# Selective scan with feed-forward: rows of B through HBM, rows of C by row quarters, a projection in column tiles, an interleaved input

## The chip, the cores and the metric

The kernel runs on one NeuronCore of a Trainium2 chip. The metric is device time in microseconds of one execution. A profile is one execution recorded instruction by instruction. TensorE (PE) does matrix products, VectorE (DVE), ScalarE (ACT) and GpSimd (POOL) work element by element, SyncE (SP) issues DMAs. SBUF is the on-chip memory of 128 partitions, PSUM the accumulator memory [...].

## What is computed

A block over x of shape (2, 1024, 512): RMS norm, a selective mask, low-rank projections, a state-space recurrence with N = 128 states for each of D = 512 features, an output projection, a layer norm, then a gated feed-forward of width 2048 and a second layer norm. All is fp32. The reference, cut:

```python
xn = x * rsqrt(mean(x * x) + 1e-06) * norm_w
xn = xn * sigmoid((xn @ select_proj_w.T + select_proj_b) * select_gate)
xp = xn @ x_proj_w.T                      # delta, B_ssm, C_ssm: 128 each
delta = softplus(xp[..., :R] @ dt_proj_w.T + dt_proj_b)
A = -exp(A_log)
h = exp(dt[:, :, None] * A) * h + (dt * xt)[:, :, None] * bt[:, None, :]   # for each token
y = einsum('bdn,bn->bd', h, ct)
x = layernorm(x + (y + x * D_param) @ out_proj_w.T)
x = layernorm(x + (silu(x @ w_gate.T) * (x @ w_up.T)) @ w_down.T)
```

## The kernel before

The 2048 tokens are cut into four chunks of T = 512 tokens, two for each sequence. For a chunk, `pre` (L114) makes the operands of the scan with features on the partitions: `xT`, `dt`, `u` = dt times the normed input, each [128, 4, 512] (the 512 features are NM = 4 groups of 128), and `b_sb`, `c_sb`, [128, 512], whose partitions are the state indices. `scan` (L212) goes through the 128 state indices n one at a time. For each n:

- `feed` (L228) is called one index ahead. `spread` (L220) puts row n of `b_sb` on all 128 partitions by a matmul with column n of the identity, broadcast, as stationary operand (L223), into the only bank of `ps_b`; ScalarE copies it to `bs` (L231); GpSimd multiplies `u` by it to make `bu` (L233), which has three buffers.
- `step` (L235) spreads row n of `c_sb` the same way into the only bank of `ps_c`. For each of the four feature groups ScalarE makes a = exp(dt times A) into PSUM (L240, two banks) and VectorE runs the recurrence along the 512 tokens with a scan instruction, in place in `bu` (L241). If another chunk of the sequence follows, GpSimd keeps the last column as state (L247). VectorE multiplies all four groups by the row of C to make `hc` (L249, two buffers).
- `reduce` (L251) is called one index late: four matmuls with the identity add `hc` to `y` (L254) in four PSUM banks.

An fp32 product appears in the profile as two MATMUL instructions and two weight loads.

After every second index one step of the neighbouring chunks' work is taken: `post` of the chunk before (L193: output projection L200, residual L203, statistics L204, layer norm L182-L191), then `pre` of the chunk after. Their PSUM tiles come from `ps_b` as well, under the same tag `b`. The calls state dependences; the framework orders the instructions of each engine from them, and every engine works its own queue in order, so that a waiting instruction holds those queued behind it. The last chunk's `post` runs alone after the scan (L305).

The feed-forward then takes the chunks in turn: `ffn_in` (L311) transposes the tokens of a chunk into `x1T` on TensorE (L110) with a copy by ScalarE (L111); for each of the 16 groups of hidden features 4 + 4 products make `pg` and `pu` (L325), whose moving operand is a row of 512 elements of `x1T`; SiLU (L329) and a product (L330) make `h`; then the down projection (L337), residual, layer norm and store. The weights `wg`, `wu`, `wd` arrive by DMA from L288, L299 and L300.

Of the kernel before, what the change touches and what calls it, by code (L numbers as in the profile page):

```python
# [9 lines left out]
FP = mybir.dt.float32  # L10
# [2 lines left out]
PSUM = bass.MemoryType.PSUM  # L13

P = 128
T = 512  # tokens of a chunk
RMS_EPS = 1e-6
LN_EPS = 1e-5
# columns of `vecs`, in groups of one column per 128 features
V_NORM, V_SELB, V_GATE, V_DTB, V_D = range(5)  # L20


# [1 line left out]
def kernel(  # L24
# [62 lines left out]
    def col(group, m):  # L87
        return vec[:, group, m : m + 1]

    # A = -exp(A_log)  # L90
    nc.scalar.activation(neg_a, neg_a, AF.Exp)
    nc.vector.tensor_scalar_mul(neg_a, neg_a, -1.0)
    nc.vector.tensor_tensor(gate_b, vec[:, V_SELB, :], vec[:, V_GATE, :], ALU.mult)
# [2 lines left out]
    state = chunk.tile([P, NM, N], FP, name="state", bufs=1)  # L96
    scan_pool = tc.alloc_tile_pool(name="scan", bufs=2)
    ps_y = tc.alloc_tile_pool(name="ps_y", bufs=1, space=PSUM)
    ps_b = tc.alloc_tile_pool(name="ps_b", bufs=1, space=PSUM)
    ps_c = tc.alloc_tile_pool(name="ps_c", bufs=1, space=PSUM)  # L100
    ps_a = tc.alloc_tile_pool(name="ps_a", bufs=2, space=PSUM)

    made = {}

    def transposed(dst, src, pool, tag, name):
        """dst[:, m, j*P:] = transposes of the blocks of src [P, NT, D]; one step for each m."""
        for m in range(NM):
            ps = pool.tile([P, T], FP, tag=tag, name=f"{name}_{m}")
            for j in range(NT):
                nc.tensor.transpose(ps[:, ts(j, P)], src[:, j, ts(m, P)], ident)  # L110
            nc.scalar.copy(dst[:, m, :], ps)  # L111
            yield

    def pre(c):  # L114
        """From the tokens of a chunk to the scan's operands, features on the partitions."""
        xT = chunk.tile([P, NM, T], FP, tag="xT", name=f"xT_{c}")
        dt = chunk.tile([P, NM, T], FP, tag="dt", name=f"dt_{c}")
        u = chunk.tile([P, NM, T], FP, tag="u", name=f"u_{c}")
        b_sb = chunk.tile([P, T], FP, tag="b_sb", name=f"b_sb_{c}")
        c_sb = chunk.tile([P, T], FP, tag="c_sb", name=f"c_sb_{c}")  # L120
        xn = pre_pool.tile([P, NM, T], FP, tag="xn", name=f"xn_{c}")
        rms = pre_pool.tile([P, T], FP, tag="rms", name=f"rms_{c}")
        low = pre_pool.tile([P, T], FP, tag="low", name=f"low_{c}")
        made[c] = xT, dt, u, b_sb, c_sb

        yield from transposed(xT, xc[c], ps_b, "b", f"tr_{c}")

        # RMS norm: a product with ones sums the squares and spreads the sum over the partitions
        nc.gpsimd.tensor_tensor(xn, xT, xT, ALU.mult)
        ps = ps_b.tile([P, T], FP, tag="b", name=f"ss_{c}")  # L130
        for k in range(NM):
            nc.tensor.matmul(ps, ones, xn[:, k, :], start=(k == 0), stop=(k == NM - 1))
        nc.scalar.activation(rms, ps, AF.Sqrt, bias=eps_r, scale=1.0 / D)
        yield
        nc.vector.reciprocal(rms, rms)
        for m in range(NM):
            nc.vector.scalar_tensor_tensor(  # L137
                xn[:, m, :], xT[:, m, :], col(V_NORM, m), rms, ALU.mult, ALU.mult
            )
        yield  # L140

        # selective mask
        for m in range(NM):
            ps = ps_b.tile([P, T], FP, tag="b", name=f"sel_{c}_{m}")
            for k in range(NM):
                nc.tensor.matmul(  # L146
                    ps, sel_w[:, k, ts(m, P)], xn[:, k, :], start=(k == 0), stop=(k == NM - 1)
                )
            nc.scalar.activation(
                dt[:, m, :], ps, AF.Identity, bias=gate_b[:, m : m + 1], scale=col(V_GATE, m)  # L150
            )
            yield
        nc.scalar.activation(dt, dt, AF.Sigmoid)
        nc.gpsimd.tensor_tensor(xn, xn, dt, ALU.mult)
        yield

        # low-rank delta, B and C
        for g, dst in enumerate((low, b_sb, c_sb)):
            ps = ps_b.tile([P, T], FP, tag="b", name=f"xp_{c}_{g}")
            for k in range(NM):  # L160
                nc.tensor.matmul(
                    ps, xp_w[:, k, ts(g, P)], xn[:, k, :], start=(k == 0), stop=(k == NM - 1)
                )
            nc.scalar.copy(dst, ps)
            yield

        # softplus(z) = max(z, 0) + ln(1 + exp(-|z|))
        for m in range(NM):
            ps = ps_b.tile([P, T], FP, tag="b", name=f"z_{c}_{m}")
            nc.tensor.matmul(ps, dt_w[:, ts(m, P)], low, start=True, stop=True)  # L170
            nc.scalar.activation(u[:, m, :], ps, AF.Relu, bias=col(V_DTB, m))
            nc.scalar.activation(dt[:, m, :], ps, AF.Abs, bias=col(V_DTB, m))
            yield
        nc.scalar.activation(dt, dt, AF.Exp, scale=-1.0)
        nc.scalar.activation(dt, dt, AF.Ln, bias=ones[:, 0:1])
        nc.gpsimd.tensor_tensor(dt, dt, u, ALU.add)
        nc.gpsimd.tensor_tensor(u, dt, xn, ALU.mult)  # L177
        yield

    def layernorm(t, stats, name):  # L180
        """Over the free dim of each of the NT rows of t, in place, from their bn_stats."""
        mv = small.tile([P, NT, 2], FP, tag="mv", name=f"mv_{name}")  # L182
        for j in range(NT):
            nc.vector.bn_aggr(mv[:, j, :], stats[:, j, :])
# [6 lines left out]
            )  # L191

    def post(c, pool, tag):  # L193
        """Output projection, residual and layer norm; the chunk's tile of x takes the result."""
        z = made[c][0]
        stats = small.tile([P, NT, 6], FP, tag="stats", name=f"stats_a{c}")
        for j in range(NT):
            ps = pool.tile([P, T], FP, tag=tag, name=f"op_{c}_{j}")
            for k in range(NM):
                nc.tensor.matmul(  # L200
                    ps, z[:, k, ts(j, P)], out_w[:, k, :], start=(k == 0), stop=(k == NM - 1)
                )
            nc.vector.tensor_tensor(xc[c][:, j, :], xc[c][:, j, :], ps, ALU.add)  # L203
            nc.vector.bn_stats(stats[:, j, :], xc[c][:, j, :])  # L204
            yield
        layernorm(xc[c], stats, f"a{c}")
        yield
# [2 lines left out]
        return t.unsqueeze(1).to_broadcast([P, NM, T])  # L210

    def scan(c, others):  # L212
        """The recurrence over a chunk, one state index at a time; `others` are steps of the
        neighbouring chunks' work, taken along the way."""
        xT, dt, u, b_sb, c_sb = made[c]
        first, last = c % CPB == 0, c % CPB == CPB - 1
        y = [ps_y.tile([P, T], FP, tag=f"y{m}", name=f"y_{c}_{m}") for m in range(NM)]
        bus, hcs = {}, {}

        def spread(pool, tag, src, n):  # L220
            """Row n of src on all partitions."""
            ps = pool.tile([P, T], FP, tag=tag, name=f"{tag}_{c}_{n}")
            nc.tensor.matmul(  # L223
                ps, ident[:, n : n + 1].to_broadcast([P, P]), src, start=True, stop=True
            )
            return ps

        def feed(n):  # L228
            ps = spread(ps_b, "b", b_sb, n)
            bs = scan_pool.tile([P, T], FP, tag="bs", name=f"bs_{c}_{n}")  # L230
            nc.scalar.copy(bs, ps)  # L231
            bus[n] = scan_pool.tile([P, NM, T], FP, tag="bu", name=f"bu_{c}_{n}", bufs=3)
            nc.gpsimd.tensor_tensor(bus[n], u, wide(bs), ALU.mult)  # L233

        def step(n):  # L235
            bu = bus.pop(n)
            cp = spread(ps_c, "c", c_sb, n)
            for m in range(NM):
                a = ps_a.tile([P, T], FP, tag="a", name=f"a_{c}_{n}_{m}")
                nc.scalar.activation(a, dt[:, m, :], AF.Exp, scale=neg_a[:, m, n : n + 1])  # L240
# [4 lines left out]
                )  # L245
            if not last:
                nc.gpsimd.tensor_copy(state[:, :, n], bu[:, :, T - 1])  # L247
            hcs[n] = scan_pool.tile([P, NM, T], FP, tag="hc", name=f"hc_{c}_{n}")
            nc.vector.tensor_tensor(hcs[n], bu, wide(cp), ALU.mult)  # L249

        def reduce(n):  # L251
            hc = hcs.pop(n)
            for m in range(NM):
                nc.tensor.matmul(y[m], ident, hc[:, m, :], start=(n == 0), stop=(n == N - 1))  # L254

        feed(0)
        for n in range(N):
            if n + 1 < N:
                feed(n + 1)
            step(n)  # L260
            if n:
                reduce(n - 1)
            if n % 2 and others:
                if next(others[0], "end") == "end":
                    others.pop(0)
        reduce(N - 1)
        for g in others:
            for _ in g:
                pass
        # z = y + x * D, in the place of x  # L270
        for m in range(NM):
            nc.vector.scalar_tensor_tensor(
                xT[:, m, :], xT[:, m, :], col(V_D, m), y[m], ALU.mult, ALU.add
# [15 lines left out]
        scan(c, others)  # L289

    ps_a.release()
    ps_c.release()
    ps_b.release()
    ps_y.release()
    scan_pool.release()
# [13 lines left out]
    ffn = ctx.enter_context(tc.tile_pool(name="ffn", bufs=2))  # L309

    def ffn_in(c):  # L311
        xT = ffn.tile([P, NM, T], FP, tag="x1T", name=f"x1T_{c}")
        for _ in transposed(xT, xc[c], ps_t, "t", f"tr1_{c}"):
            pass
        return xT
# [85 lines left out]
```

## Times and profile before

| what | value |
|---|---|
| runs without profile | 4687.51 and 4688.35 us, median 4687.93 |
| profiled execution: span, first to last instruction | 4687.7 us (no other time of that execution is recorded) |
| granted TensorE clock, mean | 0.952 |
| busy: PE, DVE, ACT, POOL | 3802.7, 3688.7, 1867.9, 2418.8 us |
| scan instructions on VectorE, L241 | 2048, 1168.3 + 1236.0 us (without and with a carried state) |
| `hc`, L249 | 512, 1166.4 us, 2278 ns each |
| `bu`, L233, on GpSimd | 512, 2312.9 us, 4521 ns each |
| `bs`, L231, on ScalarE | 512, 298.6 us, 583 ns each |
| spread of B and of C, L223 | 1024 instructions each, 573.8 and 603.0 us |
| HBM traffic | read 20.20 MB, written 4.19 MB |

How to read it: a line of a group gives line, engine, operation, names, count, busy time, mean of one in ns, and the idle time before these instructions with what ended it. A line of the timeline gives start and length in us, engine, line, operation and count, and in brackets the idle time before and its cause. A line of waits gives who waited for whom: sum in us, times, longest. The two rows of slices cut the span into 40 equal parts of 117 us; a digit is the busy share in tenths. The busy time of TensorE is modelled and overlaps; rates are better read from the starts.

### The profile page before, as it was taken

How to read it: one execution, taken by the hardware profiler on the slowest of the kernel's cores; microseconds unless marked ns; L12 is line 12 of the kernel's file. 1: busy time of each engine (PE TensorE's matmuls, PEld its weight loads, DVE VectorE, ACT ScalarE, POOL GpSimd, SP SyncE). 2: the span in 40 equal slices, each digit the busy share in tenths (PEclk: the TensorE clock that was granted, in tenths of full speed). 3: DMA queues.
4: the chain of work that ended last, by engine and by line, in shares of the span. 5: the costliest groups of instructions: out<-in, count | busy, mean ns of one | idle time of the engine just before them, and what ended most of it. 6: DMA issues, size and time to landing. Idle time of an engine off the chain costs nothing.

```text
span 4687.7 us, 25093 instructions
## 1 busy us (share of the span) xinstructions
PE 3802.7 (81%) x8224; PEld 1573.4 (34%) x8224; DVE 3688.7 (79%) x2798; ACT 1867.9 (40%) x2780; POOL 2418.8 (52%) x793
## 2 busy tenths in 40 slices
PE   5787777777787777787777777778788888999999
PEld 2333333333333333333333333333333333444444
DVE  1967999998877999998778999989999999211111
ACT  3434444443344444444345444434444444100000
POOL 3556666664545766655557666646666666000000
PEclk7988999998888999998899999989999999999999
DMA  1000000000000000000000000000000000100000
GB/s 65 0 0 0 0 0 0 0 0 0 0 0 0 0 0 0 0 0 0 0 0 36 0 0 0 0 0 0 0 0 0 0 0 0 72 9 0 9 9 9
DMA packets 9491, 25.99 MB, mean 6 GB/s; under 512 B 400, under 2 KB 912, under 8 KB 8336
## 3 DMA queue, kind: packets, MB, share of 16 engines
q1 hardware_dynamic: 9360, 24.39, 1.4%
q8 instruction: 64, 1.05, 0.1%
q14 instruction: 67, 0.55, 0.0%
HBM read 20.20 MB, written 4.19 MB: 5 GB/s over the span
## 4 chain that ended last, share of the span: by engine, by line
DVE 36%; PE 25%; issue 21%; POOL 15%; ACT 3%; DMA 0%; POOLq 0%; DVEq 0%; SPq 0%; ACTq 0%
DVE bu L241 28%; POOL bu L233 14%; DVE hc L249 6%; PE y L254 6%; PE po L337 5%; PE pg L325 5%; PE pu L325 5%; PE c L223 2%; ACT bs L231 1%; PE b L223 1%; ACT a L240 0%; PE sel L146 0%; DVE xc L189 0%; DVE xn L137 0%; POOL u L177 0%
## 5 line engine op out<-in xcount | busy, mean ns | idle before, releaser
L233 POOL TENSOR_TENSOR bu<-u,bs 128x2048 f32<-128x2048 f32 x512 | 2312.9, 4521 | 1307.8 <-ACT bs L231 735.2
L240 ACT ACTIVATE a<-dt,neg_a 128x512 f32<-128x512 f32 x2048 | 1415.6, 692 | 1854.1 <-DVE bu L241 1851.2
L254 PE MATMUL y<-hc,ident 128*128 128x512 f32 x4096 | 1931.7, 615 | 5.7 <-DVE hc L249 5.7
L241 DVE TENSOR_TENSOR_SCAN bu<-a,bu 128x512 f32<-128x512 f32 x1024 | 1168.3, 1202 | 225.0 <-POOL bu L233 224.6
L241 DVE TENSOR_TENSOR_SCAN bu<-a,state,bu 128x512 f32<-128x512 f32 x1024 | 1236.0, 1263 | 106.0 <-POOL bu L233 99.1
L249 DVE TENSOR_TENSOR hc<-bu,c 128x2048 f32<-128x2048 f32 x512 | 1166.4, 2278 | 36.1 <-PE c L223 1.2
L254 PEld LDWEIGHTS y<-hc,ident 128*128 128x128 f32 x4096 | 819.1, 200 | 1072.3 <-issue 1063.3
L223 PE MATMUL c<-c_sb,ident 128*128 128x512 f32 x1024 | 603.0, 672 | 586.5 <-DVE hc L249 586.0
L223 PE MATMUL b<-b_sb,ident 128*128 128x512 f32 x1024 | 573.8, 644 | 219.1 <-ACT bs L231 93.2
L223 PEld LDWEIGHTS c<-c_sb,ident 128*128 128x128 f32 x1024 | 167.3, 196 | 973.4 <-DVE hc L249 933.5
L231 ACT COPY bs<-b 128x512 f32<-128x512 f32 x512 | 298.6, 583 | 260.2 <-PE b L223 224.7
L223 PEld LDWEIGHTS b<-b_sb,ident 128*128 128x128 f32 x1024 | 198.3, 201 | 498.0 <-issue 206.1
L330 DVE TENSOR_TENSOR h<-sg,pu 128x512 f32<-128x512 f32 x64 | 44.0, 687 | 383.0 <-PE pu L325 383.0
L325 PE MATMUL pg<-x1T,wg 128*128 128x512 f32 x512 | 230.5, 592 | 0.0
L325 PE MATMUL pu<-x1T,wu 128*128 128x512 f32 x512 | 230.3, 592 | 0.0
L337 PE MATMUL po<-wd,h 128*128 128x512 f32 x512 | 220.9, 592 | 0.0
L329 ACT ACTIVATE sg<-pg 128x512 f32<-128x512 f32 x64 | 38.2, 597 | 376.9 <-PE pg L325 376.9
L340 DVE TENSOR_TENSOR xc<-xc,po 128x512 f32<-128x512 f32 x16 | 11.0, 688 | 202.4 <-PE po L337 202.4
L325 PEld LDWEIGHTS pu<-x1T,wu 128*128 128x128 f32 x512 | 97.3, 190 | 122.5 <-issue 122.5
L325 PEld LDWEIGHTS pg<-x1T,wg 128*128 128x128 f32 x512 | 97.1, 190 | 121.5 <-issue 121.3
L337 PEld LDWEIGHTS po<-wd,h 128*128 128x128 f32 x512 | 96.8, 190 | 119.6 <-issue 119.6
L247 POOL COPY state<-bu 128x4 f32<-128x4 f32 x256 | 50.6, 198 | 157.0 <-DVE bu L241 155.9
(62 smaller groups left out, 651.0 us busy)
## 6 DMA issues: line engine op xcount, KB each, us to landing
xc<-in_x_dram SPq DMA_DIRECT2D x4, 1024.0 KB, 12.2
wg<-in_wg_t_dram SPq DMA_DIRECT2D x1, 4096.0 KB, 12.4
wu<-in_wu_t_dram SPq DMA_DIRECT2D x1, 4096.0 KB, 13.8
wd<-in_wd_t_dram SPq DMA_DIRECT2D x1, 4096.0 KB, 24.2
out_dram<-xc SPq DMA_DIRECT2D x4, 1024.0 KB, 4.3
sel_w<-in_sel_t_dram SPq DMA_DIRECT2D x1, 1024.0 KB, 7.2
out_w<-in_out_t_dram SPq DMA_DIRECT2D x1, 1024.0 KB, 15.4
xp_w<-in_xp_t_dram SPq DMA_DIRECT2D x1, 768.0 KB, 8.9
```

The costliest lines, as they stand in the source:

```text
L223: nc.tensor.matmul(ps, ident[:, n : n + 1].to_broadcast([P, P]), src, start=True, stop=True)
L231: nc.scalar.copy(bs, ps)
L233: nc.gpsimd.tensor_tensor(bus[n], u, wide(bs), ALU.mult)
L240: nc.scalar.activation(a, dt[:, m, :], AF.Exp, scale=neg_a[:, m, n : n + 1])
L241: nc.vector.tensor_tensor_scan(bu[:, m, :], a, bu[:, m, :], 0.0 if first else state[:, m, n : n + 1], ALU.mult, ALU.add,)
L247: nc.gpsimd.tensor_copy(state[:, :, n], bu[:, :, T - 1])
L249: nc.vector.tensor_tensor(hcs[n], bu, wide(cp), ALU.mult)
L254: nc.tensor.matmul(y[m], ident, hc[:, m, :], start=(n == 0), stop=(n == N - 1))
L325: nc.tensor.matmul(ps, w[:, k, ts(f, P)], xT[:, k, :], start=(k == 0), stop=(k == NM - 1))
L329: nc.scalar.activation(sg, pg, AF.Silu)
L330: nc.vector.tensor_tensor(h[:, f, :], sg, pu, ALU.mult)
L337: nc.tensor.matmul(po, h[:, f, ts(j, P)], wd[:, f, :], start=(f == 0), stop=(f == NF - 1))
```

## The change

**Rows of B.** `pre` writes `b_sb` by DMA into a DRAM tile `b_rows` (two buffers). In the scan, `load(i)` fetches four rows, each by a DMA that reads the one row for all 128 partitions, into `bs`, now [128, 4, 512] with two buffers. The matmul and ScalarE's copy for B are gone; GpSimd multiplies from `bs`.

**Rows of C.** The states are taken in the order 0, 32, 64, 96, 1, 33, and so on. The spread uses only the 32 rows of the identity and of `c_sb` in which n lies, and two states' spreads are stated together at every even index. `ps_c` is gone; the tiles of C come from `ps_b`, which now has two banks and still serves `pre` and `post`.

**Output projection.** Each product of 128 output rows is stated as four products of 32, into the four 32-partition strips of the same bank.

**Feed-forward input.** `x1T` is laid out [128, T, NM] and seen through a rearranged view: neighbouring tokens of a feature group lie four elements (16 bytes) apart, for the copy that writes it and for the products that read it.

```diff
-    ps_b = tc.alloc_tile_pool(name="ps_b", bufs=1, space=PSUM)
-    ps_c = tc.alloc_tile_pool(name="ps_c", bufs=1, space=PSUM)
+    ps_b = tc.alloc_tile_pool(name="ps_b", bufs=2, space=PSUM)
     ps_a = tc.alloc_tile_pool(name="ps_a", bufs=2, space=PSUM)
+    rows = ctx.enter_context(tc.tile_pool(name="rows", bufs=2, space=bass.MemoryType.DRAM))
...
+        b_rows = rows.tile([N, T], FP, tag="b_rows", name=f"b_rows_{c}")
...
             nc.scalar.copy(dst, ps)
             yield
+        nc.sync.dma_start(b_rows, b_sb)
...
             for k in range(NM):
-                nc.tensor.matmul(
-                    ps, z[:, k, ts(j, P)], out_w[:, k, :], start=(k == 0), stop=(k == NM - 1)
-                )
+                for g in range(4):
+                    q = slice(g * 32, g * 32 + 32)
+                    nc.tensor.matmul(
+                        ps[q, :], z[:, k, j * P + g * 32 : j * P + g * 32 + 32], out_w[:, k, :],
+                        start=(k == 0), stop=(k == NM - 1),
+                    )
...
+        order = [g * 32 + i for i in range(32) for g in range(4)]
+
+        def load(i):
+
+            bs = scan_pool.tile([P, 4, T], FP, tag="bs", name=f"bs_{c}_{i}")
+            for g in range(4):
+                n = g * 32 + i
+                nc.sync.dma_start(bs[:, g, :], b_rows[n : n + 1, :].to_broadcast([P, T]))
+            return bs
+
+        def spread(k):
+
+            n = order[k]
+            q = slice(n // 32 * 32, n // 32 * 32 + 32)
+            cps[k] = ps_b.tile([P, T], FP, tag="b", name=f"c_{c}_{n}")
             nc.tensor.matmul(
-                ps, ident[:, n : n + 1].to_broadcast([P, P]), src, start=True, stop=True
+                cps[k], ident[q, n : n + 1].to_broadcast([32, P]), c_sb[q, :], start=True, stop=True
             )
...
+        loaded = {0: load(0), 1: load(1)}
+
+        def feed(k):
+            bs = loaded[k // 4]
+            bus[k] = scan_pool.tile([P, NM, T], FP, tag="bu", name=f"bu_{c}_{k}", bufs=3)
+            nc.gpsimd.tensor_tensor(bus[k], u, wide(bs[:, k % 4, :]), ALU.mult)
+            if k % 4 == 3 and k // 4 + 2 < N // 4:
+                loaded[k // 4 + 2] = load(k // 4 + 2)
...
         feed(0)
-        for n in range(N):
-            if n + 1 < N:
-                feed(n + 1)
-            step(n)
-            if n:
-                reduce(n - 1)
-            if n % 2 and others:
+        for k in range(N):
+            if k + 1 < N:
+                feed(k + 1)
+            if k % 2 == 0:
+                spread(k)
+                spread(k + 1)
+            step(k)
+            if k:
+                reduce(k - 1)
+            if k % 2 and others:
...
-        xT = ffn.tile([P, NM, T], FP, tag="x1T", name=f"x1T_{c}")
+        xT = ffn.tile([P, T, NM], FP, tag="x1T", name=f"x1T_{c}").rearrange("p t k -> p k t")
```

More of the change, by code (lines that the diff above doesn't have):

```diff
@@ L123, in pre @@
         low = pre_pool.tile([P, T], FP, tag="low", name=f"low_{c}")
-        made[c] = xT, dt, u, b_sb, c_sb
+        b_rows = rows.tile([N, T], FP, tag="b_rows", name=f"b_rows_{c}")
+        made[c] = xT, dt, u, b_rows, c_sb
         yield from transposed(xT, xc[c], ps_b, "b", f"tr_{c}")
@@ L212, in scan, with step @@
     def scan(c, others):
-        xT, dt, u, b_sb, c_sb = made[c]
+        xT, dt, u, b_rows, c_sb = made[c]
         first, last = c % CPB == 0, c % CPB == CPB - 1
         y = [ps_y.tile([P, T], FP, tag=f"y{m}", name=f"y_{c}_{m}") for m in range(NM)]
-        bus, hcs = {}, {}
-        def spread(pool, tag, src, n):
-            ps = pool.tile([P, T], FP, tag=tag, name=f"{tag}_{c}_{n}")
+        bus, hcs, cps = {}, {}, {}
+        order = [g * 32 + i for i in range(32) for g in range(4)]
[9 more added lines that the diff above has]
+            cps[k] = ps_b.tile([P, T], FP, tag="b", name=f"c_{c}_{n}")
             nc.tensor.matmul(
-                ps, ident[:, n : n + 1].to_broadcast([P, P]), src, start=True, stop=True
+                cps[k], ident[q, n : n + 1].to_broadcast([32, P]), c_sb[q, :], start=True, stop=True
             )
[L226 to L237, printed above, removed]
+        loaded = {0: load(0), 1: load(1)}
[5 more added lines that the diff above has]
+                loaded[k // 4 + 2] = load(k // 4 + 2)
+        def step(k):
+            bu = bus.pop(k)
+            n = order[k]
             for m in range(NM):
@@ L247, in step, with reduce @@
                 nc.gpsimd.tensor_copy(state[:, :, n], bu[:, :, T - 1])
[L248 to L252, printed above, removed]
+            hcs[k] = scan_pool.tile([P, NM, T], FP, tag="hc", name=f"hc_{c}_{n}")
+            nc.vector.tensor_tensor(hcs[k], bu, wide(cps.pop(k)), ALU.mult)
+        def reduce(k):
+            hc = hcs.pop(k)
             for m in range(NM):
-                nc.tensor.matmul(y[m], ident, hc[:, m, :], start=(n == 0), stop=(n == N - 1))
+                nc.tensor.matmul(y[m], ident, hc[:, m, :], start=(k == 0), stop=(k == N - 1))
         feed(0)
-        for n in range(N):
-            if n + 1 < N:
-                feed(n + 1)
-            step(n)
-            if n:
-                reduce(n - 1)
-            if n % 2 and others:
+        for k in range(N):
[8 more added lines that the diff above has]
+            if k % 2 and others:
                 if next(others[0], "end") == "end":
@@ L291 @@
     ps_a.release()
-    ps_c.release()
     ps_b.release()
```

## The prediction

> **What bounds the kernel now.** I read the page's slices first, then busy times by stage, then VectorE's (DVE's) waits, then the timeline. The slices show two stages: a scan in which VectorE is full or nearly so, and a tail that is all TensorE.
>
> ```profile
> PE   5787777777787777787777777778788888999999
> DVE  1967999998877999998778999989999999211111
> POOL 3556666664545766655557666646666666000000
> ```
>
> The scan runs from VectorE's first scan instruction, at 104.1 us, to about 3996; the feed-forward takes the rest, about 690 us. Inside the scan VectorE dips in slices 10-13 and 18-21, and its list of waits from 113 to 3996 us says for whom:
>
> ```profile
> DVE bu L241 <- POOL bu L233: 251.0, 94, 11.3
> DVE xT L272 <- PE y L254: 1.2, 1, 1.2
> DVE hc L249 <- PE c L223: 1.2, 2, 0.6
> ```
>
> So 251.0 us is the whole of what VectorE loses there. Between the dips it has no gap; the timeline of VectorE in the first chunk:
>
> ```profile
> 888.26 4.56 DVE L241 TENSOR_TENSOR_SCAN bu<-a,bu 128x512 f32<-128x512 f32 x4
> 892.92 2.29 DVE L249 TENSOR_TENSOR hc<-bu,c 128x2048 f32<-128x2048 f32 x1
> 895.13 4.56 DVE L241 TENSOR_TENSOR_SCAN bu<-a,bu 128x512 f32<-128x512 f32 x4
> ```
>
> One state index costs 895.13 - 888.26 = 6.87 us (6.90 in the second chunk, 1804.54 to 1811.44), all VectorE. No edit touches these instructions, so this part stays. GpSimd (POOL) needs 4.52 us for `bu` and 0.2 for the state's copy, which fits in 6.87. It is late only because of what it waits for (its own list, 113 to 4000 us):
>
> ```profile
> POOL bu L233 <- ACT bs L231: 735.2, 195, 17.1
> POOL bu L233 <- DVE hc L249: 550.6, 242, 7.3
> POOL state L247 <- DVE bu L241: 155.9, 33, 8.4
> ```
>
> The second and third are the healthy ones (a buffer or a value not due yet). The first is the chain matmul `b`, copy `bs`, product `bu`: with one bank in `ps_b`, which pre and post also use, `b` stands behind their evictions. At 1110-1125 us this is seen: TensorE waits 5.40 us for the evacuation of `op` (L203), `b` takes 2.07, `bs` 0.59, `bu` 4.50, and VectorE stands 4.41 us. In the tail TensorE has no gap:
>
> ```profile
> 4020.52 3.60 PE L325 MATMUL pg<-x1T,wg 128*128 128x512 f32 x8
> 4023.95 3.60 PE L325 MATMUL pu<-x1T,wu 128*128 128x512 f32 x8
> 4027.39 3.60 PE L325 MATMUL pg<-x1T,wg 128*128 128x512 f32 x8
> ```
>
> Eight instructions (four fp32 products, two instructions each) start 3.43 us apart: 0.429 us each. There are 1024 for gate and up: 1024 x 0.429 = 439 us, and anything that slows one of them goes straight to the end.
>
> [...] (granted 0.86-0.93 in the dips, 1.00 where the scan is steady). [...] for the 1 MB `xc` [...] the page of the profile says 12.2 to landing when all loads are issued together. I use the measured one.
>
> **The change part by part.**
>
> *Rows of B.* Out go 1024 `b` instructions, 512 copies `bs` (298.6 us of ScalarE) and the chain of POOL's first wait. In come a 256 KB write of `b_rows` and 32 loads of 1 MB per chunk, each as four DMAs on SP. A load serves four indices, 4 x 6.87 = 27.5 us, and is issued when `bu` of index 4i+3 has read the old content; `bu` of 4i+8 wants it, some four indices or 27 us later. Twice 12.2 us would still fit. SP issues took 0.37 and 0.50 us in the timeline at 3996; four per 27 us are nothing. Behind a waiting load on SP stand only the next loads, the next chunk's `b_rows` write and, in chunk 3, `wg`, needed hundreds of us later. So: hidden under POOL's and VectorE's 27 us; if that cover failed, each group of four would lose the excess. What is late next? POOL itself, in its order: pre has four products on it per chunk (18 us) that wait for ScalarE (the one at 1362 us waits 9.56 for the sigmoid, and the 11.3 us stall follows), and `hc` may now wait for `c`, which takes its two banks in turn with pre and post. Bounds: all 251 gained, or half of it. Three chunks have a pre, so I leave 20 us for each and 10 for the rest, 70: **-181**.
>
> *Rows of C by quarters.* Same count of instructions at the same 512 columns, 0.43 us each at full clock, on 32 rows. `c` of an odd index is issued up to one index early and waits for the `hc` that frees its bank; behind it in TensorE's queue is only `y`, which waits for the same `hc`. `hc` ends, `c` 1.1, `y` 3.6: done 4.7 us later, and the next `hc` wants `c` 11.4 later (6.87 + 4.56). Nothing; with half the clock for that stretch 9.4, still within. Less work for TensorE means more idle windows, but only time there is slack for.
>
> *First chunk.* With two banks, the z products (2.48 us apart at 73.5-83.4, of which ScalarE needs 1.27) and some ten others lose their 0.7-1.4 us of waiting, and two `bs` copies (0.57 each) leave the path to Ln. The write of `b_rows` follows the copy at 68.5 and even two transfers of 9.0 us (the 256 KB `dt_w`) end before POOL starts `bu` at 99.6. Bounds 0 and -15: **-10**.
>
> *Projection in 32-column tiles.* 32 instructions per row block of tokens instead of 8. No row of the trace has one. Run one by one: 13.7 us instead of 3.43. Perfectly packed: 3.43. A fp32 product is two instructions on the same strip, [...] In the last chunk, where it is on the path (14.00 us for `op` x32): **+14** (0 to +41). In the three other chunks four steps each: `y` ends 3.8 us after `hc`, the tiles at 10.7, the next `c` at 11.8, wanted at 11.4; with some half clock 2 us each, 12 x 2: **+25** (0 to about +100: one by one the next `c` comes 7-8 us late, 12 times).
>
> *Interleaved input.* Copies write at a step of 16 bytes; were each twice 0.59 us, only the first chunk's and TensorE's wait for `tr` show: **+3**. [...] Bounds 0 and +439. I take **0**, by a narrow margin.
>
> Sum: 4687.7 - 181 - 10 + 14 + 25 + 3 = 4539. The span, 4687.7, and the median of the runs, 4687.93, differ by 0.2, so the sum carries over: **4539 us**, 3.2% less.
>
> **Rivals.**
> *The interleaved read doubles gate and up* (ends slower): place, the 1024 matmuls of the tail; price 439; it decides once a read costs more than 1.55 times 0.429 (that is 243 us: 4782). For it: [...] the tail has no slack. [...] 4539 + 439 = 4978; with serial tiles 5080.
> *The read costs half as much again*: 4539 + 220 = 4759.
> *The tiles run one by one*: 4539 + (41 - 14) + (100 - 25) = 4641. [...]
> *The B chain was never the cause*, so that POOL stays late behind pre's products: the gain halves, -125 instead of -181: 4595. Against: ScalarE's copy ends 735.2 us of POOL's waits. It lies in the forecast's spread.
>
> **How the numbers follow.** Forecast 0.36 (own range 4470 to 4600), tiles one by one 0.17, half as much again 0.10, doubled 0.37 (about 0.24 at 4978, 0.13 with serial tiles). Two per cent, about what a measurement of this kernel can tell, lies at 4594 and 4782. Faster: 0.33 of the forecast and 0.05 of the serial case, 0.38. Same: 0.03 + 0.12 + 0.06 = 0.21. Slower: 0.37 + 0.04 = 0.41. For 8 in 10 the range reaches from 4470 into the doubled case, to 5000.
>
> **What would show it.** L233's wait for a copy gone, VectorE's waits in the scan near 70 us and its period still 6.87; loads landing in well under 27 us. `pg`/`pu` still 3.43 us per eight: right; 6.9: the rival. `op` in the last chunk [...] 55: serial; 14: packed. Wrong at the root would be a longer VectorE period, or `hc` waiting for `c`.

## The result and the profile after

The changed kernel takes 4912.85 us (two runs, 4912.31 and 4913.39) against 4687.93: 1.048 times as long, 95% interval 1.045 to 1.0511. Its profiled execution spans 4910.3 us, 222.6 more than before. Its lines have other numbers: L249 is `bu` on GpSimd, L259 the recurrence, L267 `hc`, L272 `y`, L240 the spread of C, L204 `op`, L345 `pg` and `pu`.

The slices of the changed kernel, now 123 us each:

```profile
PE   5888878887888788888887887887888999999999
DVE  3989999999999999999999999999995000000000
POOL 3667666656676666667666656666661000000000
```

Before, VectorE dips in slices 3-4, 10-13 and 19-22 (the prediction named the last two stretches, the second one slice early). These dips are all but gone, and the scan ends earlier. But the tail, in which only TensorE works, has grown from some 6 slices of 117 us to almost 10 of 123. The table by stage says how much (columns: stretch, length, busy us and instructions of PE, PEld, DVE, ACT and POOL, granted TensorE clock as a share of the full one, DMA share, GB/s). Before, then after, each from VectorE's first scan instruction to the end of the scan, and from there to the end:

```profile
104.10:3996.00 3891.90, 3069.26 (x6495) 1248.85 (x6496) 3595.02 (x2641) 1778.91 (x2652) 2396.28 (x779) 0.95 0.00 1
3996.00:4687.70 691.70, 681.06 (x1634) 304.44 (x1632) 87.04 (x151) 59.72 (x94) 0.00 (x0) 0.99 0.05 19
```

```profile
91.60:3733.80 3642.20, 2998.97 (x5763) 1101.41 (x5764) 3567.68 (x2640) 1495.08 (x2142) 2394.45 (x780) 0.86 0.16 38
3733.80:4910.30 1176.50, 1164.56 (x1731) 320.40 (x1729) 87.35 (x152) 66.70 (x94) 0.00 (x0) 1.00 0.03 11
```

The first scan instruction comes 12.5 us earlier (104.1 to 91.6), the scan is 249.7 us shorter (3891.9 to 3642.2), the rest 484.8 longer (691.7 to 1176.5): together the 222.6. Of the scan's gain 222.4 us are VectorE's idle time (3891.9 - 3595.0 = 296.9 before, 3642.2 - 3567.7 = 74.5 after); the other 27.3 are busy time. The clock granted in the rest is 0.99 before and 1.00 after, so a lower clock is not what made it longer. VectorE's waits of the changed kernel between 100 and 4250 us, the three that bear on the scan:

```profile
DVE hc L267 <- PE y L272: 37.8, 18, 4.6
DVE bu L259 <- POOL bu L249: 8.2, 11, 3.5
DVE bu L259 <- ACT a L258: 3.4, 3, 1.5
```

The 251.0 us of waiting for GpSimd have become 8.2. New is `hc` waiting for `y`: 37.8. The longest of these waits, with what stands before it:

```profile
252.16 2.07 PE L240 MATMUL c<-c_sb,ident 32*128 32x512 f32 x2 [4.10 <-ACT dt L150]
254.16 8.06 PE L272 MATMUL y<-hc,ident 128*128 128x512 f32 x12
259.68 2.29 DVE L267 TENSOR_TENSOR hc<-bu,c 128x2048 f32<-128x2048 f32 x1 [4.59 <-PE y L272]
```

`y` stands behind `c` in TensorE's queue (six of its instructions, whose `hc` ended at 243.67, start only at 254.16), and `c` waits for a bank that ScalarE has still to empty for `pre` (L150). All 18 waits look like this: a `c` before them waited 1.55 to 5.77 us, 13 times for ScalarE's work for `pre` and 5 times for L208, the addition that empties `op`. TensorE's timeline at the end of the scan and in the feed-forward:

```profile
3735.65 13.94 PE L204 MATMUL op<-out_w,xT 128*32 128x512 f32 x128 [0.84 <-DVE xT L293]
...
3766.77 7.38 PE L345 MATMUL pg<-x1T,wg 128*128 128x512 f32 x8
3773.97 7.38 PE L345 MATMUL pu<-x1T,wu 128*128 128x512 f32 x8
3781.17 7.38 PE L345 MATMUL pg<-x1T,wg 128*128 128x512 f32 x8
```

Eight instructions of gate or up now start 7.20 us apart (3773.97 - 3766.77), 0.900 each in place of 0.429. 1024 x 0.471 = 482 us, which is the whole growth of the tail but 3. The projection's 128 narrow instructions take 13.94 us, where 32 wide ones took 14.00 before:

```profile
3997.48 14.00 PE L200 MATMUL op<-out_w,xT 128*128 128x512 f32 x32 [0.84 <-DVE xT L272]
```

### The profile page after: what moved, and what is told of

Read it like the earlier page. It is cut to its first block, busy times and chain, and to the rows that moved or that the text cites. A ratio compares the mean times of both kernels' runs of the same rounds, so it can differ in the third digit from the quotient of the medians.

```text
span 4910.3 us, 23554 instructions
## 1 busy us (share of the span) xinstructions
PE 4209.4 (86%) x7584; PEld 1441.4 (29%) x7584; DVE 3662.8 (75%) x2798; ACT 1590.0 (32%) x2268; POOL 2416.9 (49%) x793
## 5 line engine op out<-in xcount | busy, mean ns | idle before, releaser
L249 POOL TENSOR_TENSOR bu<-u,bs 128x2048 f32<-128x2048 f32 x512 | 2311.7, 4516 | 1160.5 <-DVE hc L267 640.8
L272 PE MATMUL y<-hc,ident 128*128 128x512 f32 x4096 | 2273.4, 709 | 224.1 <-DVE hc L267 224.0
L272 PEld LDWEIGHTS y<-hc,ident 128*128 128x128 f32 x4096 | 887.7, 227 | 1646.0 <-issue 1287.3
L259 DVE TENSOR_TENSOR_SCAN bu<-a,state,bu 128x512 f32<-128x512 f32 x1024 | 1241.1, 1301 | 6.4 <-POOL bu L249 5.0
L259 DVE TENSOR_TENSOR_SCAN bu<-a,bu 128x512 f32<-128x512 f32 x1024 | 1168.8, 1203 | 67.3 <-POOL bu L249 65.3
L267 DVE TENSOR_TENSOR hc<-bu,c 128x2048 f32<-128x2048 f32 x512 | 1174.1, 2293 | 59.7 <-PE y L272 37.8
L240 PE MATMUL c<-c_sb,ident 32*128 32x512 f32 x1024 | 626.1, 707 | 438.4 <-DVE hc L267 340.7
L345 PE MATMUL pg<-x1T,wg 128*128 128x512 f32 x512 | 472.4, 1078 | 0.0
L345 PE MATMUL pu<-x1T,wu 128*128 128x512 f32 x512 | 472.4, 1078 | 0.0
L240 PEld LDWEIGHTS c<-c_sb,ident 32*128 32x128 f32 x1024 | 156.2, 192 | 827.5 <-DVE hc L267 503.2
L345 PEld LDWEIGHTS pu<-x1T,wu 128*128 128x128 f32 x512 | 106.3, 208 | 354.5 <-issue 354.5
L345 PEld LDWEIGHTS pg<-x1T,wg 128*128 128x128 f32 x512 | 106.0, 207 | 349.0 <-issue 346.9
L147 PE MATMUL sel<-xn,sel_w 128*128 128x512 f32 x128 | 58.7, 606 | 6.4 <-issue 6.4
L204 PE MATMUL op<-out_w,xT 128*32 128x512 f32 x512 | 57.6, 595 | 0.8 <-DVE xT L293 0.8
```

What stands on the lines that cost most here:

```text
L147: nc.tensor.matmul(ps, sel_w[:, k, ts(m, P)], xn[:, k, :], start=(k == 0), stop=(k == NM - 1))
L204: nc.tensor.matmul(ps[q, :], z[:, k, j * P + g * 32 : j * P + g * 32 + 32], out_w[:, k, :], start=(k == 0), stop=(k == NM - 1),)
L240: nc.tensor.matmul(cps[k], ident[q, n : n + 1].to_broadcast([32, P]), c_sb[q, :], start=True, stop=True)
L249: nc.gpsimd.tensor_tensor(bus[k], u, wide(bs[:, k % 4, :]), ALU.mult)
L259: nc.vector.tensor_tensor_scan(bu[:, m, :], a, bu[:, m, :], 0.0 if first else state[:, m, n : n + 1], ALU.mult, ALU.add,)
L267: nc.vector.tensor_tensor(hcs[k], bu, wide(cps.pop(k)), ALU.mult)
```

## The experiments

Theory: the interleaved read alone makes the kernel slower, and the loss of the chain for B makes the scan faster; the column tiles and the row quarters matter little. Rival: another part, or two parts together, give the loss, or the scan's gain has another source. Times are medians. Where no interval is given, it is one run.

**e1: the feed-forward input laid out as before.** All else as in the changed kernel.

```diff
-        xT = ffn.tile([P, T, NM], FP, tag="x1T", name=f"x1T_{c}").rearrange("p t k -> p k t")
+        xT = ffn.tile([P, NM, T], FP, tag="x1T", name=f"x1T_{c}")
```

> The changed kernel with the feed-forward input laid out as before, [128, NM, T]; the other edits stay. Theory (the step of 16 bytes doubles the read of gate and up, and nothing else of the change costs): eight gate products go from 7.20 back to 3.43 us, the copies of x1T from 1.1 to 0.59 us, and the time is 4912.9 - 1024 x (0.900 - 0.429) = 4912.9 - 482 = about 4430, 5.5% below before. Rival (the feed-forward is slow for another reason, such as the clock or DMA beside it, or the gain of the scan hangs on the layout): gate products stay above 3.5 us per eight, or the time lies above 4500.

4429.35 us, 0.9446 times before (0.9431 to 0.9462). The layout costs 4912.85 - 4429.35 = 483.5 us; the rest of the change gains 259.

```profile
3760.60 3.60 PE L345 MATMUL pg<-x1T,wg 128*128 128x512 f32 x8
3764.04 3.60 PE L345 MATMUL pu<-x1T,wu 128*128 128x512 f32 x8
```

Eight start 3.43 us apart again.

**e2: the interleaving alone**, that line in the kernel before.

> The kernel before with the interleaved feed-forward input alone. Theory: 4687.9 + 482 = about 5170, gate and up 7.20 us per eight, the scan unchanged. Rival (layout and other edits act on each other): it differs from 5170 by more than 20.

5173.69 us, 486 above before. The cost is nearly the same with and without the rest: it neither needs the other parts nor is softened by them.

**e3 and e4: the step of the read.** The four chunks get steps of 4, 8, 12 and 20 bytes (e3), and of 16, 24, 32 and 28 bytes (e4), so that one run shows four steps. In e4 `x1T` has one buffer, so only the starts inside a chunk are read there. The products take `rows_of[k]`; all else is as in e1.

```diff
+        room = ffn.tile([P, 3072], FP, tag="x1T", name=f"x1T_{c}", bufs=2)   # e4: 4096, bufs=1
+        step = (1, 2, 3, 5)[c]          # e4: (4, 6, 8, 7)
+        rows_of = []
+        for k in range(NM):
+            g, o = divmod(k, step) if step < NM else (0, k)
+            part = room[:, g * step * T : (g + 1) * step * T].rearrange("p (t s) -> p t s", s=step)
+            rows_of.append(part[:, :, o])
...
```

> The changed kernel with another step between neighbouring tokens of x1T in each chunk: 1, 2, 3 and 5 elements (4, 8, 12 and 20 bytes). Theory (a line of 16 bytes must serve at least two reads, counted in elements): per eight gate products 3.43 us at step 1 and 2, between the two at step 3 (every line serves one or two), 7.2 at step 5. Rival (each step above one element costs, since lines are only read whole): step 2 already 4.5 or more. Rival (only exact multiples of a line collide): step 5 is near 3.43.

> The changed kernel with steps of 4, 6, 8 and 7 elements (16, 24, 32 and 28 bytes) in the four chunks, one buffer of x1T instead of two. Theory (one new line per element is the worst that can be): all four read 7.2 us per eight gate products. Rival (cost grows with the step): step 8 is well above 7.2, 9 or more.

e3 4619.72 us, e4 4921.92. From e3's timeline, two lines from each chunk in order:

```profile
3850.80 3.60 PE L354 MATMUL pu<-x1T,wu 128*128 128x512 f32 x8
3854.23 3.60 PE L354 MATMUL pg<-x1T,wg 128*128 128x512 f32 x8
...
4022.18 3.76 PE L354 MATMUL pu<-x1T,wu 128*128 128x512 f32 x8
4025.78 3.76 PE L354 MATMUL pg<-x1T,wg 128*128 128x512 f32 x8
...
4246.29 5.56 PE L354 MATMUL pu<-x1T,wu 128*128 128x512 f32 x8
4251.69 5.57 PE L354 MATMUL pg<-x1T,wg 128*128 128x512 f32 x8
...
4531.24 7.47 PE L354 MATMUL pu<-x1T,wu 128*128 128x512 f32 x8
4538.53 7.47 PE L354 MATMUL pg<-x1T,wg 128*128 128x512 f32 x8
```

The starts are 3.43, 3.60, 5.40 and 7.29 us apart for 4, 8, 12 and 20 bytes. In e4 they are 7.20, 7.16, 7.34 and 7.30 for 16, 24, 32 and 28; the step of 32:

```profile
4388.26 7.52 PE L354 MATMUL pg<-x1T,wg 128*128 128x512 f32 x8
4395.60 7.52 PE L354 MATMUL pu<-x1T,wu 128*128 128x512 f32 x8
```

Call an aligned block of 16 bytes a line. A row of 512 elements touches 512 lines at steps of 16 bytes and over, 384 at 12, 256 at 8. At 7.20/(8 x 512) = 1.76 ns for a new line, 384 lines give 5.40 us for eight and 256 give 3.60: both are what was measured. At 4 bytes the element's own 0.84 ns (3.43/(8 x 512)) is the larger. So with a regular step a read costs the larger of 0.84 ns for each element and 1.76 ns for each new line, and at most 2% more (7.34 against 7.20) for a step beyond 16 bytes.

**e6: order within and between lines.** Chunk 0: pairs of neighbouring tokens (8 bytes), then a gap of 24. Chunk 1: quads of 16 bytes, then a gap. Chunk 2: alternately from two neighbouring lines (words 0, 4, 1, 5 and so on), each line used up in eight elements. Chunk 3: as before.

```diff
+        room = ffn.tile([P, NM * T], FP, tag="x1T", name=f"x1T_{c}")
+        if c == 0:
+            v = room.rearrange("p (t k i) -> p k t i", k=NM, i=2)
+        elif c == 1:
+            v = room.rearrange("p (t k i) -> p k t i", k=NM, i=4)
+        elif c == 2:
+            v = room.rearrange("p (k n j i) -> p k n i j", k=NM, j=2, i=4)
+        else:
+            v = room.rearrange("p (k t) -> p k t", k=NM)
...
```

> The changed kernel with x1T still interleaved, but in other grains by chunk: pairs of tokens (8 bytes) of a feature group side by side, then the next group; four tokens (16 bytes) side by side; contiguous rows read in the order 0, 4, 1, 5, 2, 6, 3, 7 of each eight, so that the reads change between two lines; contiguous in order. Theory (1.76 ns for each change of line, 0.84 ns for each element, the longer counts): eight gate products take 3.60, 3.43, 7.20 and 3.43 us. Rival (what counts is the step of the inner dimension or the spread of the rows): the first two are above 4. Rival (a line stays at hand once read): the third is near 3.6.

4462.38 us; eight instructions take 3.67, 3.43, 4.34 and 3.43 us. Two lines of the third chunk:

```profile
4090.31 4.50 PE L362 MATMUL pg<-x1T,wg 128*128 128x512 f32 x8
4094.64 4.51 PE L362 MATMUL pu<-x1T,wu 128*128 128x512 f32 x8
```

Pairs and quads are as the rule has it, within 2% (3.60 and 3.43). The third expectation failed: alternating between two lines costs 4.34, not the 7.20 of a new line each time. That is 4.34/(8 x 512) = 1.06 ns for each change of line, where a new line takes 1.76; a line left for longer than one element was not tried.

**e5: the four strips in turn.** e1 with the loops over k and strips exchanged, so that one strip's eight instructions stand in a row.

```diff
-            for k in range(NM):
-                for g in range(4):
+            for g in range(4):
+                for k in range(NM):
```

> The kernel of e1 with the projection's loops turned: all four k of one 32-column strip, then the next strip; same products. Theory (four strips run at once only if neighbours in the queue are of different strips; each product of 32 columns takes as long as one of 128): in the last chunk op takes 45 to 55 us instead of 13.9, and the scans with a post step lose up to 7 us each, so 4470 to 4555. Rival (a product of 32 columns is four times as short by itself): op stays at 14 us and the time at 4429.

4462.01 us. The weight loads of the projection, changed kernel first, then e5:

```profile
3736.11 0.13 PEld L204 LDWEIGHTS op<-out_w,xT 128*32 128x32 f32 x4 [0.30 <-issue]
3736.54 0.13 PEld L204 LDWEIGHTS op<-out_w,xT 128*32 128x32 f32 x4 [0.30 <-issue]
```

```profile
3755.11 0.11 PEld L204 LDWEIGHTS op<-out_w,xT 128*32 128x32 f32 x1 [0.32 <-issue]
3755.54 0.14 PEld L204 LDWEIGHTS op<-out_w,xT 128*32 128x32 f32 x3 [0.32 <-issue]
3755.97 0.14 PEld L204 LDWEIGHTS op<-out_w,xT 128*32 128x32 f32 x2 [0.29 <-issue]
3756.40 0.14 PEld L204 LDWEIGHTS op<-out_w,xT 128*32 128x32 f32 x2 [0.29 <-issue]
```

With the strips alternating, four loads come every 0.43 us: four products run at once. In turn it is 1, 3, 2, 2, two on average, and `op` in the last chunk takes 29.83 us in place of 13.94. The order in the queue decides, as the theory had it, but the size was missed (45 to 55 expected). Why two and not one run at a time is open; the time came out below the 4470 to 4555 expected. In the scan, 32 instructions now take 8.79 us, and VectorE waits 20.7 us for `op`, which it did not in e1.

**e7: C on full rows.** e1 with the spread of C from all 128 rows; order of the states and banks as in the changed kernel.

```diff
-                cps[k], ident[q, n : n + 1].to_broadcast([32, P]), c_sb[q, :], start=True, stop=True
+                cps[k], ident[:, n : n + 1].to_broadcast([P, P]), c_sb, start=True, stop=True
```

> The kernel of e1 with C spread over all 128 rows again, in the same order of states and from the same two banks. Theory (quarters of rows are off the path, TensorE has room): 4429, within 10. Rival (part of the gain is from quarters running at once): 4450 or more.

4415.45 us (0.9418, 0.9403 to 0.9434), 14 below e1. The stretch from 110 to 3650 us, e1 first, then e7 (columns as above):

```profile
110.00:3650.00 3540.00, 2906.54 (x5620) 1066.53 (x5618) 3465.19 (x2565) 1455.15 (x2084) 2330.99 (x762) 0.87 0.17 39
```

```profile
110.00:3650.00 3540.00, 2654.16 (x5641) 1056.40 (x5640) 3479.84 (x2577) 1461.29 (x2093) 2343.66 (x765) 0.92 0.17 39
```

The granted clock is 0.87 with quarters and 0.92 on full rows. With the lower clock `y` is busy 2257.7 us and not 2089.4, and VectorE's wait of `hc` for `y` is 37.2 us and not 18.6. The intervals of the two kernels just touch, but no run of one lies among those of the other (4427 to 4430, 4415 to 4417), and the wait differs the same way. So the quarters cost about 14 us here; the expectation had them off the path, within 10.

**e8: the rows of B by DMA alone**, the kernel before with that one part. B leaves `ps_b` to `pre` and `post`, C keeps its bank, the states stay in natural order; the loads of four rows are those of the change; the projection and the feed-forward input are as before.

```diff
...
-            ps = spread(ps_b, "b", b_sb, n)
-            bs = scan_pool.tile([P, T], FP, tag="bs", name=f"bs_{c}_{n}")
-            nc.scalar.copy(bs, ps)
+            bs = loaded[n // 4]
             bus[n] = scan_pool.tile([P, NM, T], FP, tag="bu", name=f"bu_{c}_{n}", bufs=3)
-            nc.gpsimd.tensor_tensor(bus[n], u, wide(bs), ALU.mult)
+            nc.gpsimd.tensor_tensor(bus[n], u, wide(bs[:, n % 4, :]), ALU.mult)
```

> The kernel before with the rows of B by DMA alone, in natural order of states; ps_b and ps_c keep one bank each, C on full rows, projection and feed-forward as before. Theory (the chain of matmul and copy behind the neighbouring chunks' evictions made GpSimd late; taking it away is the gain): VectorE's waits for L233 in the scan fall from 251 to below 60 us and the time to 4430 to 4480. Rival (the second bank that post, pre and C share is the gain): above 4550.

4378.68 us (0.9339, 0.9325 to 0.9353): 309 below before, and 51 below e1, which has this part and more. That is better than the 4430 to 4480 expected. VectorE's waits between 110 and 3650 us, and its timeline in the first chunk:

```profile
DVE bu L253 <- ACT a L252: 21.6, 10, 4.7
DVE hc L261 <- PE c L226: 5.3, 3, 2.8
```

```profile
700.74 4.55 DVE L253 TENSOR_TENSOR_SCAN bu<-a,bu 128x512 f32<-128x512 f32 x4
705.21 2.26 DVE L261 TENSOR_TENSOR hc<-bu,c 128x2048 f32<-128x2048 f32 x1
707.39 4.56 DVE L253 TENSOR_TENSOR_SCAN bu<-a,bu 128x512 f32<-128x512 f32 x4
```

No wait for GpSimd is left there. And the period is 6.65 us, not the 6.87 of before and after. In e8 the product `hc` of one index is queued behind the first scan instruction of the next; in the kernel before, in e1 and in e7 it directly follows, in the first and third chunk, the scan that writes its operand. From the first scan to `hc` are 4.47 us here and 4.66 before (888.26 to 892.92).

No line of the edit asks for this order; the framework chose it. In the traces `hc` stands directly behind its own last scan in 346 of the 512 rounds before, in 213 of the changed kernel and in 69 of e8. At 0.21 us for each (the median period of the first chunk is 6.867 before and 6.656 in e8) the 277 rounds less are worth some 58 of e8's 309 us, an estimate; most of the rest is the 251.0 of waiting.

**e9: that order in e7.** Chunks with a carried state have it already.

```diff
+                if m == 0 and pend:
+                    with tc.issue_after(ins.ins):
+                        times_c()
...
-            hcs[k] = scan_pool.tile([P, NM, T], FP, tag="hc", name=f"hc_{c}_{n}")
-            nc.vector.tensor_tensor(hcs[k], bu, wide(cps.pop(k)), ALU.mult)
+            pend.append((k, bu))
```

> The kernel of e7 (changed kernel with straight feed-forward input and C on full rows) with one more edit: the product with the row of C of index k is queued on VectorE behind the first scan instruction of index k+1 in every chunk, as e8 has it, in place of directly behind the four scans of its own index. Theory (what e8 has over e7 is this order: the product that directly follows the scan that writes its operand starts 0.2 us late): VectorE's period in the first and third chunk falls from 6.87 to 6.66 us, 0.21 x 256 = 54 us less, 4415 - 54 = 4361 us; the chunks with a carried state, which have that order already, stay at 6.90. Rival (e8 is ahead for its separate banks or its natural order of states): the period stays 6.87 and the time about 4415.

4387.75 us (0.9357, 0.9343 to 0.937). e9's timeline in the first chunk and its waits between 100 and 3600 us:

```profile
702.61 4.55 DVE L266 TENSOR_TENSOR_SCAN bu<-a,bu 128x512 f32<-128x512 f32 x4
707.08 2.25 DVE L258 TENSOR_TENSOR hc<-bu,c 128x2048 f32<-128x2048 f32 x1
709.26 4.55 DVE L266 TENSOR_TENSOR_SCAN bu<-a,bu 128x512 f32<-128x512 f32 x4
```

```profile
DVE bu L266 <- POOL bu L249: 39.2, 18, 4.6
DVE hc L258 <- PE y L281: 16.9, 13, 3.0
DVE bu L266 <- ACT a L265: 10.5, 4, 3.9
```

The period is 6.65: the order is what made it. The 54 us of the expectation were too many, since in e7 the product directly follows its scan in 209 of the 256 rounds of these chunks: some 44 us, of which 28 reach the end. The wait for GpSimd has grown from e7's 15.6 to 39.2, that for `a` from 4.5 to 10.5.

**e12: a fourth buffer of `bu` in e9.**

```diff
-            bus[k] = scan_pool.tile([P, NM, T], FP, tag="bu", name=f"bu_{c}_{k}", bufs=3)
+            bus[k] = scan_pool.tile([P, NM, T], FP, tag="bu", name=f"bu_{c}_{k}", bufs=4)
```

> The kernel of e9 with four buffers of bu in place of three; nothing else. In e9 the period fell to 6.66 us as expected but the time only by 28 of 54 us, and VectorE's wait for the product on GpSimd in the first and third chunk grew from about 8 to 33 us. Theory (the product with C ends one scan later, so it frees its buffer of bu later, and three buffers no longer give GpSimd the lead that covers the work of the neighbouring chunks): with a fourth buffer that wait falls below 12 us and the time to about 4388 - 22 = 4366 us. Rival (GpSimd is late by its own queue, in which the products of pre stand, whatever the buffers): wait and time stay, 4388 within 5.

4350.98 us (0.9274, 0.9259 to 0.929), the fastest of all. The same waits:

```profile
DVE hc L258 <- PE y L281: 14.2, 14, 2.3
DVE bu L266 <- POOL bu L249: 14.0, 11, 3.5
DVE bu L266 <- ACT a L265: 4.0, 3, 1.4
```

The wait for GpSimd is back at 14.0 (below 12 was expected): `hc`, ending one scan later, had held `bu` too long. The three waits together fell by 34 us (66.6 to 32.2), the time by 37. e8 has the late order with three buffers and no wait for GpSimd, so the late order alone does not need the fourth; that it takes the shared banks of C as well is likely, but not shown.

**e10: quarters for C in e8.**

```diff
-                ps, ident[:, n : n + 1].to_broadcast([P, P]), src, start=True, stop=True
+                ps, ident[n // 32 * 32 : n // 32 * 32 + 32, n : n + 1].to_broadcast([32, P]),
+                src[n // 32 * 32 : n // 32 * 32 + 32, :], start=True, stop=True
```

> The kernel of e8 (before with only the rows of B by DMA) with the rows of C spread from quarters of 32 rows; banks and order as in e8. Theory (a spread on 32 rows earns a lower granted TensorE clock, which makes y and c later; e7 against e1 gave 14 us): granted clock over the scan near 0.87 in place of 0.94 or so, time 5 to 20 us above e8's 4378.7. Rival (the 14 us came from the shared banks, in which a quarter's spread starts too early or too late): clock and time as e8, 4378.7 within 3.

4384.09 us (0.9349, 0.9334 to 0.9365). From 110 to 3650 us e10's granted clock is 0.90, e8's 0.94: the quarters lower it here too, without shared banks, though not to the 0.87 expected. The 5 us between the two times lie within their intervals, and `hc` waits for `c` 6.8 us against 5.3. So the lower clock is shown twice; that it costs time is shown only with the shared banks, in e7.

**e11: two banks alone.** The kernel before with B, C, `pre` and `post` sharing two banks, and nothing else.

```diff
-    ps_b = tc.alloc_tile_pool(name="ps_b", bufs=1, space=PSUM)
-    ps_c = tc.alloc_tile_pool(name="ps_c", bufs=1, space=PSUM)
+    ps_b = tc.alloc_tile_pool(name="ps_b", bufs=2, space=PSUM)
...
-            cp = spread(ps_c, "c", c_sb, n)
+            cp = spread(ps_b, "b", c_sb, n)
...
```

> The kernel before with nothing changed but the banks: the pool of C is gone and B, C, pre and post share two banks under one tag; B still goes by matmul and ScalarE's copy. Theory (what costs VectorE 251 us is the chain of matmul, copy and product for B behind other work on TensorE and ScalarE, and only taking B off that chain frees it): above 4600 us, VectorE's wait for the product on GpSimd still above 150 us. Rival (the single bank is what makes the chain late, and a second bank alone brings most of the gain): about 4450 us, that wait below 60 us.

4722.23 us, 34 above before. VectorE's waits from 150 to 3990 us:

```profile
DVE bu L240 <- POOL bu L232: 178.7, 148, 8.8
DVE hc L248 <- PE b L222: 68.1, 36, 3.6
DVE bu L240 <- ACT a L239: 18.6, 46, 2.4
```

Sharing the two banks does not free the chain; C now waits in it too. The gain comes from taking B off TensorE and ScalarE. A second bank for B beside C's own was not tried; the kernel before has eight banks in use (`y` four, `a` two, B and C one each), and the changed kernel as many.

## Why the prediction was wrong, step by step

**Interleaved input: the step that failed.** The 0 in the sum means that a new line for each element costs no more than the element itself. It costs more: 1.76 ns for a new line against 0.84 for an element, so that each of the 1024 instructions went from 0.429 to 0.900 us: +482 where the sum had 0. Two elements per line cost 3.60 against 3.43 us for eight instructions, one costs 7.20, as e3's theory has it. A fixed time for each line fits these numbers as well; all operands here are fp32, so the two cannot be told apart. The rival "doubles" had the right place; its 439 was short by 43, since 1.76 ns is more than twice 0.84. A term with bounds 0 and +439, in a stage without slack, was set to 0 by an estimate of the author that no row of the trace supported. The prediction's own chances had the doubling (0.37) level with its forecast (0.36). With the doubling and all else as forecast it had 4978; the measured span is 68 less, because the tail cost 43 more and the rest came out 110 better.

**Rows of B: right mechanism, gain too small.** POOL's wait for the copy and the 251.0 us are gone, as said; the loads of 256 KB land 5.4 us after issue (median of 512), within the 27 us. The term left 70 us for POOL behind `pre`'s products and for a `c` whose banks `pre` and `post` hold. The first came to 8.2; the second is the 37.8 of `hc` behind `y`, in which `c` is late for its bank just as the prediction feared; waiting for `a` adds 3.4. Predicted for the scan: -181 + 25 = -156. Measured: -249.7, of which 251.0 - 49.4 = 201.6 is in these waits. The other 48 us, 20.8 of them idle and 27.3 busy time, the prediction had at nothing: it called the 251.0 the whole of VectorE's loss, where the stage has 296.9 us of idle time, and took the period as fixed. But in the last chunk the period falls from 7.12 to 6.90 us (two indices from 3503.10 to 3517.34 before, 3502.14 to 3515.93 after), and over all chunks `hc` directly follows its own scan in 133 rounds fewer (346 to 213), which at 0.21 us is 28 us, an estimate; the remaining 20 are open. Elsewhere the period stayed at 6.87, as said, but that is no floor: 6.65 was to be had by order (e8, e9).

**First chunk: right.** -10 predicted, -12.5 measured. It belongs to the two banks: e8, without them, has its first scan at 103.68; e11, which has nothing else, at 91.33.

**Projection: wrong, in favour of the change.** The +14, an estimate of the author, put `op` at some 28 us in the last chunk; 13.94 came. Four strips that alternate are fully packed even with two instructions a product: 128 narrow ones took 13.94 us, 32 wide ones 14.00. The +14 was 0. Of the +25 at most 5 were there: VectorE does not wait for `op` in the scan, and the five waits of `hc` behind a `c` that waited for L208 sum to 5.0 us.

**C by quarters: "Nothing" was near.** About 14 us (e1 to e7), with a lower granted clock and a later `y`. The step had `c`, `y` and even a halved clock, 9.4 us against 11.4, but no wait for the bank: in the case shown with the result `c` takes 2.07 us (1.12 at 245.88), but it also waits 4.10 us for its bank, and `hc` then 4.59 us for `y`.

**Copies of the input:** they went from 587 to 1100 ns, as the step's "twice" supposed; with all else around the products, the tail grew 3 us beyond the 482.

Taken together: 4687.7 - 12.5 - 249.7 + 484.8 = 4910.3. The scan went 94 us better than forecast, the first chunk 2.5 and the projection at the end 14; the tail's 482 outweigh all of it.

## What to carry to other kernels

Before a moving operand of TensorE is laid out with a step, count the new 16-byte lines that a row touches: here every one cost 1.76 ns against 0.84 for an element, so two fp32 neighbours per line were nearly free (3.60 us for eight instructions against 3.43) and one per line doubled the time (7.20) of products that had no slack behind them. A row broadcast that goes through a matmul, a copy and a contended bank can be taken off two engines by a DMA from HBM: here that gained 309 us, the order of instructions that came with it included (e8). On a full engine look at the order of dependent instructions: an instruction that directly followed its producer began 0.2 us late (`hc` 4.66 us after the first scan, and 4.47 with another scan between), in 209 of 256 rounds here, and moving it gained 28 us, with one more buffer 64.

## What was not expected of the hardware

- Alternating between two lines, element by element, cost 4.34 us for eight instructions (e6), between the 3.43 of contiguous reads and the 7.20 of a new line for each element.
- Four 32-column strips in alternation did an fp32 projection in 13.94 us, as fast as full width (14.00); the same instructions strip after strip took 29.83 (e5), two at a time on average.
- Spreading from 32 rows instead of 128 lowered the granted clock over the scan, 0.92 to 0.87 and 0.94 to 0.90, though as many instructions run over the same 512 columns.
- A ScalarE copy of 512 elements per partition that writes at a step of 16 bytes took 1100 ns, a contiguous one 587.
